# Storing transposed keys through SyncE with the output stores, and two full products placed between the last half-size products

## Chip, core and metric

The kernel runs on one core of a Trainium2 chip. The metric is the device time of one execution in microseconds. Three timed runs of the kernel before gave 1010.33, 1010.59 and 1010.79 us, median 1010.59.

## What is computed

The input `x` is 2 sequences of 2048 tokens of 512 elements in float32. Cut to what matters, the reference is:

```python
xn = layernorm(x)
z  = layernorm(xn) * gamma + beta                  # inside the attention
q, k, v = z @ qkv[:, :512], z @ qkv[:, 512:1024], z @ qkv[:, 1024:]
attn = softmax(causal(q @ k.T / sqrt(512)))        # each sequence by itself
s  = (attn @ v) @ o_proj + xn
top2 of (xn @ gate_w.T + gate_b + bias) over 8 experts, softmax of the two
y  = sum over the two: gate * (silu(xn @ w1[e].T + b1[e]) @ w2[e].T + b2[e])
out = x + s * silu(y)
```

## The kernel before

**Stages.** The work falls into three stages on one core. The first, 0 to 251 us in the profile, makes normalized tokens, keys, projected queries and projected values, and decides the routing to the experts. The second runs the experts over gathered tokens. The third is the causal attention with the gated output. The change touches the first stage only.

**Weights folded.** q and k appear only in q @ k.T, so the kernel forms `wqk`, the product of the query and key weights, once, and applies it to the transposed normalized tokens. These transposed tokens are what the program calls keys, `kT`. In the same way `wvo` is the product of the value weights and the output projection.

**Blocks.** The 4096 tokens are 8 blocks of 512 tokens. Of each block the first stage makes `kT` (four chunks of 128 x 512), a projected q and a projected v, and stores all three in DRAM (`kt_d`, `qt_d`, `v_d`), from where the attention reads them from 527 us on. The rows of a block are normalized on DVE, copied by POOL into 16-bit halves (`zu`), transposed by DMAs on SP's queue (`zuT`, L354), stored for the experts' gathers (`zu_d`, L357), and put together again by DVE as `zT` (L374); block 0 is transposed by PE instead. ACT then makes `kT` of `zT` in four steps (`scaled`, L379), and after the last of them issues one store of 1 MB from its own queue (L384). There are four `kT` buffers and one `zT` buffer.

**Products by seven.** Blocks 0 to 6 are projected with a scheme of seven half-size products for each q and each v, in place of eight. An item is the q or the v of one block, so there are 14 items, (0, q), (0, v), (1, q) and so on. `one_product(i, k)` (from L504) issues the eight 256-column matmuls of product k of item i (all at L526) and the ACT copies that follow it. The scheme accumulates in PSUM banks and passes partial sums between banks with ACT: product 1 goes to bank a, product 5 to bank d and from there to SBUF as the "fifth", product 2 adds to bank a, product 6 to bank b, which ACT copies to bank c (L555). Product 3 then adds to bank b, product 7 to bank c, and after bank c has been copied out (L539), product 4 adds to bank c. Two DVE adds per item (L395) bring the fifth to what products 3 and 7 gave; `deferred` holds an add back until two more products have been issued.

**Units.** Block 7 is projected with eight full products instead, the units (`unit(b, u)`, L439): four 512-column matmuls (L446 for q, L451 for v) into bank `(u + 1) % 4`, an ACT copy (L456) and an ACT store of 256 KB (L457).

**Order.** All engines run in the order in which the program issues. `chain_of_products` fixes the order of the products, interleaving an item with the next; of the last item only products 3, 7, 4 are left at the end, one directly after another. `pieces` is a generator that issues products and gives control back four times in seven products, 56 times in all, and then once per unit, 8 times. At each of these 64 steps other work is issued: `norm_*`, `keys`, gate products (`both`, L412) and their transposes (L427), loads of x and of the experts' weights, and from step 41 on the parts of `route`, the routing on DVE with its inversion matmuls on PE (`inv_p`, L746). `made` counts products; `scale_next` issues one waiting `scaled` step after a product. Stores of q and v of an item wait in the list `unstored` and are issued at the next product 3 (L577), through SP for blocks 0 to 4 and through ACT for blocks 5 and 6, or after a unit.

**SP's queue.** SP issues in one order the transposes, the `zu_d` stores, the loads of x and weights, and the q and v stores of blocks 0 to 4. An issue that has to wait holds up all those behind it.

Of the kernel before, what the change touches and what calls it, by code (L numbers as in the profile page):

```python
# [26 lines left out]
def gated_attention_moe(  # L27
# [28 lines left out]
    nc = tc.nc  # L56
    B, S, D = x.shape
    E, _, H = w1_t.shape
# [6 lines left out]
    ND = D // P  # L65
# [32 lines left out]
    kt_d = [dram.tile([P, ND, TB], F32, name=f"kt_d{b}") for b in range(NB)]  # L98
# [50 lines left out]
    banks = [ps_p.tile([P, TB], F32, name=f"bank_{k}", tag=f"bank_{k}") for k in "abcd"]  # L149
# [212 lines left out]
    def keys(b):  # L362
        zs = zs_of.pop(b)
        zT = ztp.tile([P, ND, TB], F32, name=f"zT_{b}", tag="zT")
        kT = kp.tile([P, ND, TB], F32, name=f"kT_{b}", tag="kT")
        if b < BY_TE:
            for c in range(ND):
                pt = ps_t.tile([P, TB], F32, name=f"pz_{b}_{c}", tag="pt")
                for t in range(BT):
                    nc.tensor.transpose(pt[:, ts(t, P)], zs[t][:, ts(c, P)], ident)  # L370
                nc.scalar.copy(zT[:, c, :], pt)
        else:
            for t in range(BT):
                nc.vector.tensor_copy(  # L374
                    zT[:, :, ts(t, P)].bitcast(U16).rearrange("p c (t h) -> p c t h", h=2),
                    zuts.pop((b, t)).rearrange("p (h c) t -> p c t h", h=2),
                )
        def scaled(c):
            nc.scalar.activation(  # L379
                kT[:, c, :], zT[:, c, :], AF.Identity,  # L380
                scale=gam[:, c : c + 1], bias=bet[:, c : c + 1],
            )
            if c == ND - 1:
                nc.scalar.dma_start(out=kt_d[b], in_=kT)  # L384

        wait = made[0] + {1: 3, NB - 1: 4}.get(b, 6)
        pending.extend((wait, scaled, c, b) for c in range(ND))
        kts[b], zts[b] = kT, zT

    made, pending, deferred = [0], [], []  # L390

    def add_due(wait=2):
        while deferred and deferred[0][0] + wait <= made[0]:
            _, f, args = deferred.pop(0)
            f(*args)  # L395

    def scale_next():
        if pending and pending[0][0] <= made[0]:
            _, f, c, _ = pending.pop(0)
            f(c)  # L400
# [38 lines left out]
    def unit(b, u):  # L439

        kT = kts[b]
        po = banks[(u + 1) % ND]
        r = u % ND
        for c in range(ND):
            if u < ND:
                nc.tensor.matmul(  # L446
                    po, lhsT=wqk[:, c, ts(r, P)], rhs=kT[:, c, :],
                    start=(c == 0), stop=(c == ND - 1),
                )
            else:  # L450
                nc.tensor.matmul(  # L451
                    po, lhsT=kT[:, c, ts(r, P)], rhs=wvo[:, c, :],
                    start=(c == 0), stop=(c == ND - 1),
                )
        o = stg.tile([P, TB], F32, name=f"j_{b}_{u}", tag="stg")
        nc.scalar.copy(o, po)  # L456
        nc.scalar.dma_start(out=(qt_d if u < ND else v_d)[b][:, r, :], in_=o)  # L457
# [4 lines left out]
    SEVEN = NB - 1  # L462
# [30 lines left out]
    items = [(b, of_q) for b in range(SEVEN) for of_q in (True, False)]  # L493
    FIFTH = {}

    def chain_of_products():
        yield from ((0, k) for k in (1, 5, 2, 6))
        for i in range(len(items)):
            more = i + 1 < len(items)
            for j, k in (1, 1), (0, 3), (0, 7), (1, 5), (0, 4), (1, 2), (1, 6):  # L500
                if j == 0 or more:
                    yield i + j, k

    def one_product(i, k):  # L504

# [61 lines left out]
        else:  # L567
# [1 line left out]
            nc.scalar.copy(place(1, 0), whole(bank_c))  # L569
            queue = nc.sync if b < LATE else nc.scalar  # L570
            unstored.extend(((qt_d if of_q else v_d)[b], g, outs[:, g], queue) for g in range(2))

    unstored = []

    def store(dst, g, src, queue):

        queue.dma_start(out=dst[:, 2 * g : 2 * g + 2, :], in_=src)  # L577
# [262 lines left out]
    units = [(b, u) for b in range(NB) for u in range(2 * ND)]  # L840
# [70 lines left out]

    def pieces():

        for n, (i, k) in enumerate(chain_of_products()):
            made[0] = n
            add_due()
            one_product(i, k)
            scale_next()
            if (n + 1) * 4 // 7 > n * 4 // 7:
                units.pop(0)  # L920
                yield
        while units:
            add_due(0)
            unit(*units.pop(0))
            while unstored:
                store(*unstored.pop(0))
            yield

    def sum_keys(i):
# [3 lines left out]
        elif i % (2 * ND) == 4 and b < SEVEN - 1:  # L933
            if b == 1:
                scale_all()
            key_sums(b)

    projected = pieces()
    for i in range(LAST + 1):
        next(projected)  # L940
# [347 lines left out]
    def maximum(s, src, at):  # L1288

        mx, _, pieces = scored[s]  # L1290
        nc.vector.tensor_reduce(mx[:, len(pieces) : len(pieces) + 1], src, AX.X, ALU.max)  # L1291
        pieces.append((src, at))
# [96 lines left out]
    def end_scores(s):  # L1389
        mx, nm, pieces = scored[s]  # L1390
        nc.vector.tensor_reduce(nm, mx[:, : len(pieces)], AX.X, ALU.max, negate=True)  # L1391
# [7 lines left out]
    while w2_left:  # L1399
# [12 lines left out]
        out=keep, in_=keep, compare_op=ALU.is_ge, fill=-HUGE,  # L1412
        base=0, pattern=[[-1, P]], channel_multiplier=1,
    )
    for i in range(NM):
# [21 lines left out]
        for _ in range(3):  # L1437
            if i >= paired.stop and early:
                f, b, c = early.pop(0)
# [316 lines left out]
    for s in range(NT + OUT + 2):  # L1756
# [7 lines left out]
        n = s // 2 + 1  # L1764
# [172 lines left out]
```

## Time and profile before

| what | value |
|---|---|
| median of the timed runs | 1010.59 us |
| time of the profiled execution | 1012.02 us |
| its span | 1010.3 us |
| granted PE clock | 1.00 |
| PE busy | 1001.5 us, 99% |
| DVE, POOL, ACT busy | 71%, 48%, 40% |
| waits of PE in the first 251 us | six, 4.2 us together |
| issues of kt_d stores | 8 on ACT, 1 MB each, 0.33 us each |

The profile is of one execution. Its rows name a line of the program, an engine, an operation, the tiles written and read (out<-in), the number of instructions, and the time. A timeline row begins with the start in us from the span's start and the duration; what stands in brackets at its end is the idle time of the engine before it, and whose work ended it. "ACTq" and "SPq" are those engines' sequencers, which issue DMAs. A wait row gives who waited for whom, the total in us, the number of times, and the longest. Ends of matmuls are modelled.

### The profile page before, as it was taken

Reading aid. Unit: us, or ns where it says so; the run is one execution under the profiler, and the core shown is the slowest. Engines: PE = TensorE matmul, PEld = TensorE weight load, DVE = VectorE, ACT = ScalarE, POOL = GpSimd, SP = SyncE. Lnnn points to the kernel's source line nnn. Section 1 sums busy time; section 2 is a strip of 40 time slices with the busy share of each in tenths; the row PEclk is TensorE's granted clock in tenths of the full one; section 3 lists DMA queues with packets and bytes.
Section 4 is the critical chain, followed back from the end, with each engine's and each line's share of the span. In section 5 each row is a group of like instructions: output and inputs, shape, how many; then the busy total and the mean of one; then the engine's idle time right before and its main releaser. Section 6 shows DMA issues by size and latency. Waiting matters only on the chain. (4 is left out here: it accounts for less than half of the span.)

```text
span 1010.3 us, 13408 instructions
## 1 busy us (share of the span) xinstructions
PE 1001.5 (99%) x3924; PEld 665.7 (66%) x3924; DVE 719.6 (71%) x1396; ACT 402.7 (40%) x804; POOL 481.6 (48%) x475
## 2 busy tenths in 40 slices
PE   9999999999999999999999999999999999999998
PEld 5887888874577677667653448677675544447577
DVE  6997755896877777776744669678576457878667
ACT  3354455322444544444455122232345544442241
POOL 4474465003744444443432256164557776764272
PEclk9999999999999999999999999999999999999999
DMA  8799987979999999999999576373677768753361
GB/s 291 234 240 319 319 237 268 331 254 230 182 247 213 205 219 218 210 211 214 213 213 254 162 191 149 90 189 110 186 199 233 224 202 241 204 146 86 95 164 42
DMA packets 295495, 207.96 MB, mean 206 GB/s; under 512 B 230648, under 2 KB 243704, under 8 KB 294400
## 3 DMA queue, kind: packets, MB, share of 16 engines
q1 hardware_dynamic: 280128, 155.17, 62.1%
q0 software_dynamic: 10400, 34.63, 12.6%
q10 hardware_dynamic: 4896, 17.30, 4.6%
q8 instruction: 34, 0.56, 0.2%
q14 instruction: 37, 0.30, 0.1%
HBM read 92.35 MB, written 60.03 MB: 151 GB/s over the span
## 5 line engine op out<-in xcount | busy, mean ns | idle before, releaser
L1191 PE MATMUL py<-arena,ht 128*128 (+3 forms) x396 | 176.7, 593 | 0.0
L1303 PE MATMUL ps<-k,q 128*128 128x512 f32 (+3 forms) x416 | 143.0, 495 | 0.3 <-PEq L1451 0.3
L1491 POOL COPY pu<-pT 128x1024 uint16<-128x1024 uint16 (+2 forms) x74 | 81.8, 1137 | 119.1 <-ACT pT L1481 59.2
L1162 POOL COPY hu<-h 128x704 uint16<-128x704 uint16 x66 | 61.8, 954 | 155.8 <-issue 121.7
L1191 PEld LDWEIGHTS py<-arena,ht 128*128 128x128 f32 (+3 forms) x396 | 71.8, 185 | 80.6 <-issue 76.4
L1303 PEld LDWEIGHTS ps<-k,q 128*128 128x128 f32 x416 | 74.7, 190 | 67.1 <-issue 56.3
L966 POOL DMA_INDIRECT xs<-zu_d,toki x66 | 77.7, 1177 | 70.6 <-DVE toki L793 55.9
L1177 ACT ACTIVATE ht<-ht,b1sel 128x128 f32<-128x128 f32 (+3 forms) x216 | 67.9, 380 | 88.4 <-DVE ht L1171 88.4
L1141 DVE TENSOR_TENSOR h<-p,h 128x176 f32<-128x176 f32 x182 | 55.4, 336 | 59.6 <-PE p L1134 56.1
L1674 POOL DMA_INDIRECT yg<-y_d,posi x64 | 67.3, 1052 | 36.9 <-DVE yg L1685 22.0
L1531 PE MATMUL po<-v,pT 128*128 128x512 f32 x152 | 67.9, 592 | 0.0
L347 POOL COPY zu<-z 128x1024 uint16<-128x1024 uint16 x32 | 39.4, 1230 | 57.7 <-DVE z L332 57.7
L1481 ACT ACTIVATE pT<-pT,nm 128x1024 f32<-128x1024 f32 x14 | 16.1, 1148 | 110.3 <-DVE nm L1391 72.0
L1513 DVE COPY pT<-puT 128x1024 uint16<-128x1024 uint16 (+2 forms) x74 | 53.4, 750 | 7.4 <-DMA puT<-pu 7.2
L1199 ACT COPY y<-py 128x512 f32<-128x512 f32 x55 | 32.1, 584 | 62.1 <-PE py L1191 48.2
L1481 ACT ACTIVATE pT<-ps,nm 128x512 f32<-128x512 f32 (+3 forms) x52 | 30.0, 580 | 60.4 <-DVE nm L1391 36.7
L1361 DVE TENSOR_TENSOR pT<-p,pT 128x512 f32<-128x512 f32 x49 | 32.9, 687 | 25.8 <-PE p L1355 22.1
L1531 PEld LDWEIGHTS po<-v,pT 128*128 128x128 f32 x152 | 28.6, 190 | 31.9 <-issue 30.1
L1042 DVE COPY xT<-xhT 128x1024 uint16<-128x1024 uint16 x66 | 44.7, 703 | 6.4 <-DMA xhT<-xs 6.3
L1703 POOL TENSOR_TENSOR o<-o,yg 128x512 f32<-128x512 f32 x30 | 41.4, 1380 | 14.3 <-DVE o L1695 14.2
L1695 DVE SCALAR_TENSOR_TENSOR o<-xo,xscale,o 128x512 f32<-128x512 f32 x30 | 25.9, 871 | 30.1 <-ACT o L1692 30.1
L1704 POOL TENSOR_TENSOR o<-o,xo 128x512 f32<-128x512 f32 x30 | 43.2, 1439 | 2.4
(342 smaller groups left out, 2146.9 us busy)
## 6 DMA issues: line engine op xcount, KB each, us to landing
y_d<-y SPq DMA_DIRECT2D x66, 256.0 KB, 4.3
zu_d<-zu SPq DMA_DIRECT2D x32, 264.0 KB, 3.2
kt_d<-kT ACTq DMA_DIRECT2D x8, 1024.0 KB, 8.2
q<-qt_d SPq DMA_DIRECT2D x32, 256.0 KB, 5.0
k<-kt_d SPq DMA_DIRECT2D x32, 256.0 KB, 4.2
v<-v_d SPq DMA_DIRECT2D x32, 256.0 KB, 5.7
xo<-in_x_dram SPq DMA_DIRECT2D x32, 256.0 KB, 4.0
x<-in_x_dram SPq DMA_DIRECT2D x30, 256.0 KB, 6.5
```

The costliest lines, as they stand in the source:

```text
L966: nc.gpsimd.indirect_dma_start(out=xs, out_offset=None, in_=zu_d, in_offset=bass.IndirectOffsetOnAxis(ap=toki[:, order[i] : order[i] + 1], ...
L1042: nc.vector.tensor_copy(xT.bitcast(U16).rearrange("p c (t h) -> p c t h", h=2), xhs.pop(i).rearrange("p (h c) t -> p c t h", h=2),)
L1141: nc.vector.tensor_tensor(out, x, y, ALU.add)
L1162: nc.gpsimd.tensor_copy(hu[:, :, :H], h.bitcast(U16).rearrange("p (d h) -> p h d", h=2))
L1177: nc.scalar.activation(ht[:hn, c, at], ht[:hn, c, at], AF.Silu, bias=b1sel[:hn, c, j : j + 1])
L1191: nc.tensor.matmul(py[at, :], lhsT=ht[:k, c, at], rhs=rhs[n], start=(c == 0), stop=(c == NH - 1),)
L1303: nc.tensor.matmul(ps[:, :w], lhsT=aqs[seq[s] // 2][:, c, ts(t % 2, P)], rhs=aks[first + j][:, c, :w], start=(c == 0), stop=(c == ND - 1),)
L1481: nc.scalar.activation(turned[s][:, at:end], src, AF.Exp, bias=nm, accum_out=rs[:, j : j + 1])
L1491: nc.gpsimd.tensor_copy(pu[:, : 2 * w].rearrange("p (h d) -> p h d", h=2), turned[s][:, k : k + w].bitcast(U16).rearrange("p (d h) -> p h ...
L1513: nc.vector.tensor_copy(turned[s][:, k : k + w].bitcast(U16).rearrange("p (i t h) -> p i t h", t=P, h=2), puT[:, : 2 * w // P, :].rearrang ...
L1531: nc.tensor.matmul(dst, lhsT=turned[s][:, ts(k, P)], rhs=avs[first + k // BT][:, k % BT, cols], start=(start and k == k0), stop=(k == k1 - 1),
L1674: nc.gpsimd.indirect_dma_start(out=y, out_offset=None, in_=y_d, in_offset=bass.IndirectOffsetOnAxis(ap=posi[k][:, n : n + 1], axis=0),)
```

## The change

Three things are different. First, `scaled` no longer issues the 1 MB store on ACT; it puts two stores of 512 KB into `unstored`, to be issued by SP together with the next q and v stores, whatever the block. Second, `chain_of_products` yields `None` twice among the products of the last item, ahead of its product 3 and ahead of its product 4; at each `None`, `pieces` issues the next unit of block 7 and gives control back. The products themselves and their number stay. Third, a unit uses bank `(u + 3) % 4`, so that unit 0 goes to bank d and unit 1 to bank a. The counter `n` is kept by hand, since units no longer all follow the products.

```diff
             if c == ND - 1:
-                nc.scalar.dma_start(out=kt_d[b], in_=kT)
+                unstored.extend((kt_d[b], g, kT[:, 2 * g : 2 * g + 2, :], nc.sync) for g in range(2))
...
-    made, pending, deferred = [0], [], []
+    made, pending, deferred, unstored = [0], [], [], []
...
-        po = banks[(u + 1) % ND]
+        po = banks[(u + 3) % ND]
...
     def chain_of_products():
         yield from ((0, k) for k in (1, 5, 2, 6))
-        for i in range(len(items)):
-            more = i + 1 < len(items)
+        for i in range(len(items) - 1):
             for j, k in (1, 1), (0, 3), (0, 7), (1, 5), (0, 4), (1, 2), (1, 6):
-                if j == 0 or more:
-                    yield i + j, k
+                yield i + j, k
+        for k in (None, 3, 7, None, 4):
+            yield len(items) - 1, k
...
-    unstored = []
...
-        for n, (i, k) in enumerate(chain_of_products()):
+        n = 0
+        for i, k in chain_of_products():
+            if k is None:
+                unit(*units.pop(next(j for j, (b, _) in enumerate(units) if b == SEVEN)))
+                yield
+                continue
             made[0] = n
             add_due()
             one_product(i, k)
             scale_next()
-            if (n + 1) * 4 // 7 > n * 4 // 7:
+            n += 1
+            if n * 4 // 7 > (n - 1) * 4 // 7:
                 units.pop(0)
                 yield
```

## The prediction

> **What bounds the kernel now.** I read the page first (engine totals, slices), then the waits of PE, then the timelines of PE, ACT, SP and DVE around each wait that the change touches.
>
> ```profile
> PE 1001.5 (99%) x3924; PEld 665.7 (66%) x3924; DVE 719.6 (71%) x1396; ACT 402.7 (40%) x804; POOL 481.6 (48%) x475
> ```
> ```profile
> PE bank_a L526 <- ACT raw L552: 1.4, 1, 1.4
> ...
> PE bank_b L526 <- ACT bank_c L555: 0.7, 1, 0.7
> PE inv_p L746 <- DVE which L779: 0.4, 1, 0.4
> ...
> PE bank_c L526 <- ACT so L539: 0.3, 1, 0.3
> ```
>
> PE is the bound in every stage: 99% busy at full clock, so only PE work or a PE wait is worth time. The change leaves the matmuls as they are; it can only move waits. All waits of PE are eight lines with one occurrence each, 4.9 us in all, and these four lie in the first 251 us, where the changed code runs. After 251 us PE has two waits, 0.4 us for DVE's work on PE's own results and 0.3 us of its own sequencer, so what PE gains before 251 us should reach the end.
>
> The listed idle understates a wait, because a product is drawn 1.89 us long while the next starts 1.73 us later (the tail overlaps). I price a wait by starts against the same pair elsewhere:
>
> ```profile
> 80.99 0.60 PE L427 MATMUL pgt<-ident,part 128*128 128x128 f32 x4
> 82.99 1.99 PE L526 MATMUL bank_a<-kT,wqk 128*128 128x256 f32 x8 [1.40 <-ACT raw L552]
> ...
> 212.72 1.89 PE L526 MATMUL bank_b<-arena 128*128 128x256 f32 x8
> 215.32 1.99 PE L526 MATMUL bank_b<-arena,kT 128*128 128x256 f32 x8 [0.71 <-ACT bank_c L555]
> 217.16 1.89 PE L526 MATMUL bank_c<-arena 128*128 128x256 f32 x8
> 218.88 0.64 PE L746 MATMUL inv_p<-which,at 128*128 128x136 bf16 x8
> 219.78 1.99 PE L526 MATMUL bank_c<-wvo,arena 128*128 128x256 f32 x8 [0.26 <-ACT so L539]
> ...
> 225.57 0.64 PE L746 MATMUL inv_p<-which,at 128*128 128x136 bf16 x8
> 226.63 0.63 PE L746 MATMUL inv_p<-which,at 128*128 128x136 bf16 x8 [0.43 <-DVE which L779]
> ```
>
> Without a wait, a product follows a gate transpose (L427) after 0.44 us (101.55 to 101.99), a product a product after 1.73, a product or an inversion an inversion after 0.47 (204.24 to 204.71). So the four cost 2.00 - 0.44 = **1.56**, 2.60 - 1.73 = **0.87**, 0.90 - 0.47 = **0.43** and 1.06 - 0.47 = **0.59** us.
>
> The first needs ACT's timeline:
>
> ```profile
> 76.49 0.81 ACT L379 ACTIVATE kT<-zT,bet,gam 128x512 f32<-128x512 f32 x1
> 81.49 0.33 ACTq L384 DMA_DIRECT2D kt_d<-kT  x1
> 81.86 0.58 ACT L569 COPY raw<-bank_c 128x512 f32<-128x512 f32 x1 [4.55 <-PE pgt L427]
> ```
>
> Block 2's keys were complete at 77.30, yet ACT issued their store at 81.49 and copied nothing meanwhile. PE L427 is not what it waited for: L384 reads nothing from PE. The trace's semaphore records show ACT held until 81.43 by one of eight DMA completion counters that SP and ACT use in turn; the last transfer on that counter was the third zu store, issued by SP at 77.05, last piece landed at 81.41 (SP's four x loads after it took 4.71 us to issue, against 1.79 at 24.9). PE's product needed bank_a, whose copy stands right behind the held one (82.34 to 82.94). So ACT paid for SP's congested queue, and PE for ACT.
>
> **The Trainium skill.** "PSUM — Partial Sum Buffer", Engine vs sequencer instructions: ScalarE's queue is strict FIFO. The trace agrees: the finished bank_c product waited for its copy until L384 was out (81.82, copy 81.86). Same page, PSUM bank collisions: a bank is guarded as a whole between TensorE and its reader; that is the 0.87 and 0.43 above. "DMA: Bandwidth & Descriptors", Issuing engines are not separate DMA queues: SP's and ACT's transfers share 16 engines, so moving the issuer saves only issue time. The trace agrees: from 85 to 86 us ACT's queue moved 385 KB and SP's 37. Same page, Rules for kernel authors: at least 1 MiB per DMA for full bandwidth. Here the halves do not show a loss: two 512 KB qt halves landed 1.30 us apart (72.03, 73.33), about 400 KB/us, as fast as the 1 MB stores.
>
> **Part 1: key stores moved to SP.** Removed from ACT: 8 issues of 0.33 us (2.6 us of an engine 40% busy, hidden by its idle time) and the one hold of 4.1 us, which is worth 1.56 us of PE. The other seven L384 issues follow their keys at once, so nothing is there to gain. Added to SP: 16 issues of 512 KB, at 0.58 us each (median of the L577 row) 9 us over 130 us. SP waits 53 us there for POOL's zu alone, so the issue time hides; without that cover it would delay the transposes by 1.2 us a block. Same bytes, 8 MB. A key buffer is written again four blocks later: block 1's (store landed near 75 at worst) at 131.4, so that wait stays hidden.
>
> What the stores are moved past is the question. They leave at the next third product of the chain, behind what SP has before it: block 0's store goes from 26.26 to about 62 (behind zuT and zu_d of block 2), block 1's from 53.56 to about 67, block 2's from 81.49 to about 96. So 2 MB more stand ahead of block 3's transposes (67.51 to 75.89). At the 390 KB/us that the trace's packets show in undisturbed stretches that is 5.4 us; at the 235 KB/us over 64.8 to 73.3 (2 MB landed) it is 8.9. The last zuT of block 3 landed at 79.41: it becomes 84.8 to 88.3, and with one copy of 0.7 to 1.7 us zT is ready at 85.5 to 90.0. PE's gate product of block 3 (L412, 88.37 before) would come at 86.8. Cost 0 to 3.2 us; nothing below zero, as PE cannot start it earlier. I take 0, since block 1's store also leaves the queue at 54 to 57 and SP's issue is spread. From block 4 on the zT copies wait for ACT (97.96, with zuT landed at 95.74), and block 2's 1 MB has left the stretch 81 to 89, so the backlog is repaid.
>
> **Part 2: two units between the last products.** Nothing is removed: the same 8 units of block 7 run, two of them earlier. Unit 0 goes on bank_d (read out at 209.5), unit 1 on bank_a (213.5), so both start at once; each covers 3.49 us. In the clock of before: unit 0 at 214.45, inversion 217.94, products 218.41 and 220.14, inversion 221.87, unit 1 222.34, inversions 225.83 and 226.30, last product 226.77, unit 2 at 228.5. Product 3 needs ACT's bank copy (done 215.3), product 4 the copy of bank_c (about 222.5): 0.87 and 0.43 go, covered by the units. The inversion wait goes too: its `which` needed 3.2 us after the inversion at 221.61 and an add of 0.69 (222.73) stood before it; now it starts at 222.4 without the add and is ready at 225.7, before 226.30. Next late is nothing on PE. Extra changes of operand shape: up to 0.1 us, taken as 0.
>
> Moved with them: two ACT copies and two qt_d stores (0.33 each), ACT being idle over 1 us before each product's copy, and block 6's two qt_d stores, which leave at the third product, 3.1 us later; nobody reads them before 527. Block 7's keys were complete at 170. The counter of products, by which adds fall due, doesn't count units. W2's last loads wait for products 7 and 4, so SP issues them at 222 and 228.6 instead of 219.08 and 221.80; SP's next transpose starts at 232.30 in any case. First expert product: xT was joined at 242.45, needed at 249.2.
>
> The add of product 7 now falls behind the router's DVE block:
>
> ```profile
> 222.73 0.69 DVE L395 TENSOR_TENSOR so<-so,p 128x512 f32<-128x512 f32 x1
> ...
> 227.31 0.30 DVE L788 COPY inv<-inv_p 128x136 f32<-128x136 f32 x1 [0.72 <-PE inv_p L746]
> ```
>
> That block lasts 14.29 us (to 241.60, the end of DVE L833); starting at 227.0 the add ends near 242.0. The second v_d store waits for it on ACT, from about 232.5, and behind it the copies of units 3 to 5. Unit 7 needs unit 3's bank at 245.7, and the copy ends near 243.0: 2.7 us to spare, cost 0.
>
> **Sum.** 1.56 + 0.87 + 0.43 + 0.59 = 3.45 us. The profiled execution: 1012.02 (span 1010.3 plus 1.7 around it) - 3.45 = 1008.57. The three timed runs have a median 1.43 below the profiled time, so **1007.1**. Within 0.2% (2.0 us) is about what a measurement here can't tell from no change.
>
> **Rivals.**
> - *Backlog or no stall to save*: the 1.56 is given back at L412, or the timed runs don't have it (the 1.43 between profile and median would fit). For: DMA share over 1.0 from 60 to 110 us. Against: three runs within 0.46 us. Gain 1.89: 1008.7.
> - *Tail shifted, not gained*: `which` is ready only 0.6 us before its use; if the inversions wait there again, and the backlog takes the 1.56, a third of the tail's 1.89 is left, 0.6: 1010.0. For: DVE is over 90% busy there. Against: DVE's work moves with PE's, and an add falls out of its way.
> - *Slower, by ACT parked*: the second v_d store, at 242.0, also has to get a completion counter. If that wait is over 2.7 us, unit 7 stands still. The longest of this kind is SP's 8.1:
>
> ```profile
> SPq L955 <- DMA v_d<-arena: 8.1, 1, 8.1
> ```
>
>  That costs 5.4 us, net +1.95: 1012.5. Against: ACT met such a hold once in its 24 stores.
>
> **Chances.** Full gain 0.50 (own range 1006.5 to 1007.8); backlog 0.27; shifted 0.11; slower 0.12. Faster by over 0.2%, below 1008.6: the first and 0.12 of the second, 0.62; within 0.2%: 0.15 + 0.11 = 0.26; slower 0.12. Range: 1006.5 to 1010.2 leaves out the slower case and a little of the others.
>
> **What would show it.** ACT has no gap at 77 to 82 and PE no wait for bank_a; PE's waits lose L555, L539 and L779; unit 0 and 1 appear on bank_d and bank_a among the last products; a v_d store leaves ACT near 240. I am wrong if PE waits for zT at L412, or for a unit's copy before 250 us, or if the four waits go and the span does not follow.

## The result, and the profile after

The changed kernel took 1008.2 us (median of 10 runs, 1007.43 to 1008.87), beside 1010.75 us for the kernel before (10 runs, 1010.33 to 1013.08). The ratio is 0.997 with a 95% interval of 0.9962 to 0.9978: faster by 2.55 us by the medians and by 3.0 by the ratio. The forecast was 1007.1 with a range of 1006.5 to 1010.2: the direction and the range held, and the point was 1.1 us too low. The profiled execution of the changed kernel took 1007.83 us with a span of 1006.0, where the one before took 1012.02 and 1010.3.

The engine totals on the page after:

```profile
PE 999.9 (99%) x3924; PEld 665.3 (66%) x3924; DVE 716.9 (71%) x1396; ACT 403.2 (40%) x804; POOL 483.3 (48%) x475
```

PE has the same 3924 matmuls and is as full as before. All of its waits (who waited for whom, total, times, longest) are now four:

```profile
PE warm L870 <- DVE b1s L181: 1.1, 1, 1.1
PE p L1583 <- DVE u L1600: 0.4, 1, 0.4
PE ps L1307 <- PEq L1455: 0.3, 1, 0.3
PE pz L370 <- ACT zT L371: 0.3, 1, 0.3
```

The four that the prediction priced are gone, and no new one took their place. PE's timeline after shows the two places:

```profile
80.43 0.60 PE L427 MATMUL pgt<-ident,part 128*128 128x128 f32 x4
80.87 1.89 PE L526 MATMUL bank_a<-kT,wqk 128*128 128x256 f32 x8
...
86.15 1.06 PE L412 MATMUL pg<-zT,gw 128*32 128x512 f32 x8
...
212.23 3.60 PE L446 MATMUL bank_d<-kT,wqk 128*128 128x512 f32 x8
215.66 0.64 PE L744 MATMUL inv_p<-which,at 128*128 128x136 bf16 x8
216.13 1.94 PE L526 MATMUL bank_b<-arena,kT 128*128 128x256 f32 x8
217.91 1.89 PE L526 MATMUL bank_c<-arena 128*128 128x256 f32 x8
219.64 0.64 PE L744 MATMUL inv_p<-which,at 128*128 128x136 bf16 x8
220.11 3.65 PE L446 MATMUL bank_a<-kT,wqk 128*128 128x512 f32 x8
223.60 1.11 PE L744 MATMUL inv_p<-which,at 128*128 128x136 bf16 x16
224.54 1.94 PE L526 MATMUL bank_c<-wvo,arena 128*128 128x256 f32 x8
...
243.49 3.60 PE L451 MATMUL bank_c<-wvo,kT 128*128 128x512 f32 x8
```

The product into bank_a follows the gate transpose by 0.44 us, where it took 2.00. The gate product that might have met the backlog (L412) starts at 86.15 with no wait in brackets. In the tail the units stand on bank_d and bank_a, and every start follows the one before it within 0.06 us of what the sum had drawn: the two inversions at 223.60 run as one group of 16 matmuls. Unit 7, the last, starts at 243.49.

ACT's timeline after, first around the keys of block 2, then around the parked v_d store:

```profile
75.94 0.82 ACT L379 ACTIVATE kT<-zT,bet,gam 128x512 f32<-128x512 f32 x1
77.18 0.59 ACT L569 COPY raw<-bank_c 128x512 f32<-128x512 f32 x1 [0.43 <-PE bank_c L526]
78.91 0.59 ACT L552 COPY raw<-bank_a 128x512 f32<-128x512 f32 x1 [1.14 <-PE bank_a L526]
...
230.95 9.05 ACTq L575 DMA_DIRECT2D v_d<-so  x2
240.05 0.59 ACT L456 COPY j<-bank_c 128x512 f32<-128x512 f32 x1 [9.51 <-DVE so L395]
```

Copies now follow the keys within half a microsecond; before, ACT stood from 77.30 to 81.49. And ACT is parked in the tail: it stands at the two v_d stores for 9.05 us, 8.3 of them waiting for DVE's add (`so`, L395) as foreseen; its copy of unit 3 (bank_c) ends at 240.64, and unit 7 needs that bank at 243.49.

**Where the time went.** I compared the start of each matmul with its start before. The two profiled spans differ by 4.3 us: 0.55 in the first 7 us, 1.67 at the bank_a product and 2.05 in the tail; after that the offset stays the same to the end. The first part is no work of the change. PE's timelines of before and then of after, at the first products with weights:

```profile
4.06 2.08 PE L225 MATMUL bank_a<-raw 128*128 128x512 f32 x2
5.92 1.19 PE L225 MATMUL bank_b<-raw 128*128 128x512 f32 x2
```
```profile
4.18 1.51 PE L225 MATMUL bank_a<-raw 128*128 128x512 f32 x2
5.53 1.02 PE L225 MATMUL bank_b<-raw 128*128 128x512 f32 x2
```

Within these rows PE waits for nothing; the matmuls themselves come closer together in the changed kernel. The third follows the second after 0.85 us before and after 0.43 in the changed kernel. The record of the granted clock in the traces begins full speed at 6.25 us in the one and at 5.00 in the other. In the fourteen executions profiled for this document that moment lies between 4.17 and 7.34 us, and the fifth of these matmuls starts between 5.92 and 7.54, the later the later full speed begins (correlation 0.997). The same program differs in this too: 6.25 and 5.60 us in the two executions of before. So the change itself is worth 1.67 + 2.05 = 3.72 us in this pair of profiles (3.45 predicted), and 2.55 to 3.0 in the timed runs.

### The profile page after: what moved, and what is told of

It is laid out like the page before. It is cut to its first block, busy times and chain, and to the rows that moved or that the text cites. A ratio compares the mean times of both kernels' runs of the same rounds, so it can differ in the third digit from the quotient of the medians.

```text
span 1006.0 us, 13431 instructions
## 1 busy us (share of the span) xinstructions
PE 999.9 (99%) x3924; PEld 665.3 (66%) x3924; DVE 716.9 (71%) x1396; ACT 403.2 (40%) x804; POOL 483.3 (48%) x475
## 5 line engine op out<-in xcount | busy, mean ns | idle before, releaser
L1365 DVE TENSOR_TENSOR pT<-p,pT 128x512 f32<-128x512 f32 x49 | 32.9, 687 | 25.8 <-PE p L1359 22.1
```

## The experiments

**The theory** is the prediction's: key stores on ACT now and then wait for a DMA completion counter that SP's transfers still hold (called a hold below), which stops ACT's copies and through them PE; and the units cover three waits in the tail. **Rivals**: the gain is all in one part; it is the later time or the half size of the key stores that helps, not the issuer; ACT's parking in the tail is itself a cost or a danger.

### Each part alone, and the kernel before again

keys_only is the kernel before with only the key stores moved (units stay at the end); units_only is the changed kernel with the store back on ACT (the units keep their new banks, which no run tried apart):

```diff
-                unstored.extend((kt_d[b], g, kT[:, 2 * g : 2 * g + 2, :], nc.sync) for g in range(2))
+                nc.scalar.dma_start(out=kt_d[b], in_=kT)
```

block2_only moves only the one store that was held, and before_again is the kernel before with nothing changed, for a second profile.

```diff
-                nc.scalar.dma_start(out=kt_d[b], in_=kT)
+                if b == 2:
+                    unstored.extend((kt_d[b], g, kT[:, 2 * g : 2 * g + 2, :], nc.sync) for g in range(2))
+                else:
+                    nc.scalar.dma_start(out=kt_d[b], in_=kT)
```

keys_only: 

> Only the key stores go to SP with the next output stores; units stay behind the last product. Theory (one hold of ACT behind block 2's store, 1.6 us of PE): 1.6 us faster than before, PE's wait for bank_a gone, the three waits of the tail (0.7, 0.3, 0.4 us listed) still there. Rival (the hold was a chance of the one profiled execution): 0 to 0.5 us faster when timed. Rival (SP's backlog costs something elsewhere): PE waits at the gate products of blocks 3 to 5, slower than before.

units_only: 

> Only the two units move between the last products, on the new banks; the key stores stay on ACT. Theory: 2.0 us faster than before (0.87 + 0.43 + 0.59 by the starts of before, 2.05 by those of after), bank_a's wait near 82 us still there in the profile. Rival (the whole timed gain comes from here, as the hold was a chance): as fast as the changed kernel, 2.6 to 3 us.

block2_only: 

> The kernel before, with block 2's key store alone moved to SP behind the next output stores; the other seven stay on ACT. Theory (only that store was ever held): 1.6 us faster, as keys_only, and no wait of PE for ACT before 200 us. Rival (ACT's issues cost in every block): clearly less than keys_only. Rival (the hold passes to another of ACT's stores, since the order of the completion counters shifts): a new wait of PE at another block, 0 to 1 us faster.

before_again: 

> The kernel before, unchanged, one more execution with a profile. Theory: PE waits again for bank_a near 82 us, 1 to 2 us, and the three waits of the tail return within 0.1 us. Rival (the hold was a chance): no wait for bank_a, and a span about 1.5 us shorter.

| kernel | median us (runs) | before beside it | ratio, 95% interval | span of the profile |
|---|---|---|---|---|
| keys_only | 1009.92 (14) | 1010.95 | 0.9998, 0.9986 to 1.001 | 1008.5 |
| units_only | 1009.05 (13) | 1010.95 | 0.9981, 0.9973 to 0.9989 | 1007.4 |
| block2_only | 1010.36 (13) | 1010.95 | 0.9994, 0.9986 to 1.0002 | 1008.7 |
| before_again | 1011.14 (1) | | | 1009.4 |

The units alone gain 1.9 us, as the sum for the tail had it (1.89). keys_only is undecided: its median is 1.0 us lower, but four of its fourteen runs took 1012 to 1016 us and pulled the ratio to 1; of the 35 runs of before beside it, four took 1012 to 1013. In its profile the wait for bank_a is gone and the tail's three waits are still there. block2_only is undecided too; its profile has no bank_a wait either, and before 200 us no wait for ACT but the 0.3 us at `pz` that every profile has, so in this execution none of the other seven stores cost PE anything. It lost 0.1 us at 122 us and some 0.5 at the experts' entrance, where DVE waits 3.4 us for a transpose (`huT`), against 2.7 before; why that landed later I did not trace.

The useful finding came from the profiles that keep the stores on ACT. ACT's timeline in units_only:

```profile
80.60 0.33 ACTq L384 DMA_DIRECT2D kt_d<-kT  x1
80.97 0.58 ACT L569 COPY raw<-bank_c 128x512 f32<-128x512 f32 x1 [3.93 <-PE bank_b L526]
```

The hold is there again at the same store. PE's product starts 1.37 us after the gate transpose (80.72 to 82.09) and in before_again 1.34 (80.77 to 82.11), so the hold costs 0.93 and 0.90 us there, against 1.56 in the profile that the prediction was made from. It is there in all three profiles that have block 2's store on ACT at its old place. By the semaphore records of all three, ACT waits for the same counter, last used by the third zu store of SP, and is released within 0.03 us of that store's last landing: at 81.41, 80.54 and 80.52 us. The size of the hold changes from execution to execution, and the first profile had a large one.

### The keys alone once more

keys_again repeats keys_only on another chip.

> The kernel with the key stores alone moved, a second time, since four of its 14 runs lay over 1012 and left the interval at no verdict. Theory: 0.9 to 1.2 us faster than before (the hold of PE was 0.9 in two of three profiles of kernels with ACT's stores, 1.6 in the third). Rival (the moved stores bring a slow case of their own): again a quarter of the runs over 1012, which the kernel before shows in a seventh.

It took 1010.35 us in 22 runs (1009.41 to 1011.07) beside 1011.2 in 27 runs: 0.999, interval 0.9984 to 0.9997. The key stores are worth about 0.9 to 1.0 us, which agrees with a cost of 0.90 to 0.93, or 1.0 with the slower start after the wait (below). The runs over 1012 us did not come back. The two parts add up: 1.0 + 1.9 = 2.9, against 2.55 to 3.0 for both.

### Issuer, delay or half size

sp_at_once is the kernel before with the same 1 MB store at the same place in the program, on SP instead of ACT. act_later is the changed kernel with late half stores, but issued by ACT:

```diff
-                nc.scalar.dma_start(out=kt_d[b], in_=kT)
+                nc.sync.dma_start(out=kt_d[b], in_=kT)
```
```diff
-                unstored.extend((kt_d[b], g, kT[:, 2 * g : 2 * g + 2, :], nc.sync) for g in range(2))
+                unstored.extend((kt_d[b], g, kT[:, 2 * g : 2 * g + 2, :], nc.scalar) for g in range(2))
```

sp_at_once: 

> The kernel before, with each block's 1 MB key store issued by SP in the place where ACT issued it, not later and not in halves. Theory (the issuer matters, since SP's own holds lie beside PE's work): no wait of PE for bank_a, 0.9 to 1.6 us faster than before, as keys_only. Rival (SP reaches the store before the keys are there, waits for ACT, and block transposes queue behind it): PE waits at gate products, 0 to 3 us slower than before.

act_later: 

> The changed kernel, with the key stores still in halves and still at the next product 3, but issued by ACT. Theory (the issuer matters): ACT is held again at one or more of these stores by a completion counter that SP's transfers use, and PE waits 0.3 to 2 us somewhere in 60 to 170 us. Rival (the later place is what helps, whoever issues): no such wait, as fast as the changed kernel.

sp_at_once took 1010.11 us (20 runs) beside 1011.19: 0.9987, interval 0.998 to 0.9993, the gain of the keys without delay and without halves. Its PE has no wait for bank_a, although SP now stands waiting for keys (PE's timeline, and waits of SP's queue):

```profile
80.96 0.60 PE L427 MATMUL pgt<-ident,part 128*128 128x128 f32 x4
81.39 1.89 PE L526 MATMUL bank_a<-kT,wqk 128*128 128x256 f32 x8
```
```profile
SPq L384 <- ACT kT L379: 6.6, 2, 4.6
```

PE lost some 0.5 us at the experts' entrance instead, in a wait of 0.2 for ACT's `ht`, as in block2_only.

act_later took 1014.01 us (13 runs) beside 1011.19: 1.0027, interval 1.0016 to 1.0038, slower than the kernel before although it keeps the gain of the tail. ACT's timeline there, and then PE's:

```profile
59.22 0.57 ACT L560 COPY bank_b<-bank_a 128x512 f32<-128x512 f32 x1
63.06 1.23 ACTq L575 DMA_DIRECT2D kt_d<-kT  x2
64.33 0.59 ACT L539 COPY raw<-bank_c 128x512 f32<-128x512 f32 x1 [4.53 <-DMA zu_d<-zu]
```
```profile
60.13 1.89 PE L526 MATMUL bank_d<-arena 128*128 128x256 f32 x8
64.97 1.99 PE L526 MATMUL bank_c<-wvo,arena 128*128 128x256 f32 x8 [2.95 <-ACT raw L539]
```

Here the bracket itself names the cause: what ended ACT's 4.53 us was a landing of `zu_d`, a store issued by SP that has nothing to do with the keys. PE starts 4.84 us after the product before it instead of 1.73: 3.1 us lost, and 1.0 more at 106 us, where the counter was last used by a qt_d store of SP. With 0.1 for the slower start after each wait the two make 4.3 of the 4.9 us between its span (1010.9) and that of the changed kernel; 0.3 more is the first matmuls' clock and 0.3 a gate transpose at 171 us. So the gain needs neither delay nor half size, and on ACT the same late halves are worse. The issuer is the cause.

### The parked store: how far from harm, and what if it is not parked

In the tail ACT is parked behind the second v_d store, which waits for DVE's add. add_late delays that add by filler work on DVE ahead of the remaining units; add_early issues the add ahead of the router's work, so that the store is not parked:

```diff
+        for _ in range(17):
+            nc.vector.tensor_tensor(sc, sc, sc, ALU.min)
         while units:
```
```diff
             one_product(i, k)
+            if (i, k) == (len(items) - 1, 4):
+                add_due(0)
             scale_next()
```

add_late: 

> The changed kernel, with 17 more operations of DVE (a minimum of the routing scores with themselves, which changes nothing, about 0.4 us each, 6.8 us in all) between the router's last DVE block and the add of product 7. Theory (from 2.85 us on, each us that the add is later stops PE at unit 7): PE waits about 3.9 us for a unit's copy near 244 us, span 3.9 us longer than the changed kernel's. Rival (ACT has more room than that, or the first experts' tokens, joined by DVE behind the add, decide): 0 to 1.5 us longer, with PE's wait at the first expert product.

add_early: 

> The changed kernel, with the add of the last item's product 7 issued right behind product 4, ahead of the router's last DVE block. Theory (ACT's 9 us behind the second v_d store lie inside unit 7's slack of 2.85 us): ACT's hold from 230.95 to 240.00 is gone, PE's schedule is the same, the time that of the changed kernel within 0.3 us. Rival (the parked ACT costs something that the waits of PE don't list): 0.3 to 1 us faster than the changed kernel.

add_late took 1016.82 us (4 runs, 1015.28 to 1019.74; the profiled one is the shortest) beside 1011.19: 1.0059, interval 1.0038 to 1.0079. Its timelines of ACT and of PE, and PE's last windows (length; busy us of PE, PEld, DVE, ACT and POOL with instructions; granted clock share; DMA share; GB/s):

```profile
231.78 16.75 ACTq L575 DMA_DIRECT2D v_d<-so  x2
248.57 0.58 ACT L456 COPY j<-bank_c 128x512 f32<-128x512 f32 x1 [17.20 <-DVE so L395]
```
```profile
240.88 3.60 PE L451 MATMUL bank_b<-wvo,kT 128*128 128x512 f32 x8
249.21 5.36 PE L451 MATMUL bank_c<-wvo,kT 128*128 128x512 f32 x8 [4.73 <-ACT j L456]
254.41 7.85 PE L1088 MATMUL ph<-w,xT 128*128 x26
```
```profile
249.00:256.00 7.00, 6.79 (x14) 3.33 (x15) 1.73 (x3) 2.50 (x5) 1.14 (x3) 0.76 0.78 262
```

This execution runs 0.82 us behind the changed kernel's ahead of the filler (240.88 against 240.06). Counted from there, ACT's copy comes 7.7 us later and unit 7 starts 4.9 later, so the first 2.8 us of delay are free; the prediction had 2.7 to spare. The mechanism of the slower rival is real, and the changed kernel stands 2.8 us from it. Beyond that the price is more than the wait: the experts' first product comes 6.7 us later, 1.8 more than the 4.9, because PE came out of the wait at a reduced rate (window row, clock 0.76; unit 7 drawn as 5.36 us instead of 3.60). The expectation of 3.9 us in all did not foresee this.

add_early took 1008.68 us (10 runs, 1007.62 to 1010.56) beside 1011.19: 0.9973, interval 0.9963 to 0.9983. That is not better than the changed kernel's 0.997, and its runs spread: five lie between 1007.6 and 1008.3, three between 1010.1 and 1010.6, two between these. Its profile is of a long one (1010.38). ACT's timeline, and PE's wait:

```profile
231.61 1.76 ACTq L575 DMA_DIRECT2D v_d<-so  x2
...
240.93 0.59 ACT L456 COPY j<-bank_a 128x512 f32<-128x512 f32 x1 [2.85 <-PE bank_a L451]
249.97 0.33 ACTq L457 DMA_DIRECT2D v_d<-j  x1
250.39 0.59 ACT L456 COPY j<-bank_b 128x512 f32<-128x512 f32 x1 [8.88 <-PE ph L1088]
```
```profile
PE py L1197 <- ACT ht L1183: 1.4, 2, 1.0
```

The long park at 231 is gone, and ACT stands 8.4 us later on: the store behind the copy of 240.93 leaves at 249.97. By the trace's semaphore records its counter belonged to one of SP's transposes of the experts' tokens, issued at 234.97 and landed at 249.9. Behind it ACT comes late to the experts' activations, and PE loses 2.0 us at 258 and 264. The five transposes are slower there, too; SP's queue in the changed kernel, and in add_early:

```profile
229.93 11.76 SPq L1041 DMA_TRANSPOSE xhT<-xs  x5
```
```profile
230.45 19.72 SPq L1043 DMA_TRANSPOSE xhT<-xs  x5
```

### Both once more

> The kernel with the early add, unchanged, one more execution with a profile. Its ten timed runs lay half near 1008 and half near 1010. Theory (a hold of ACT behind a store of block 7 near 241 to 250 us, present in some executions, makes the difference): near 1008 without the hold and without a wait of PE for ht, or near 1010 with both. Rival: near 1010 with no hold, or near 1008 with one.

> The changed kernel, unchanged, one more execution with a profile. Theory: PE has no wait for bank_a, bank_b, bank_c and inv_p, the tail is as in the first profile within 0.1 us, and what differs in the span lies in the first 7 us, where the weights arrive. Rival (other holds of ACT come and go in it, as in add_early): a wait of PE for ht or a bank of 0.5 to 2 us.

Each ran once more. add_early_again took 1010.55 us, again a long one, and ACT's timeline again has the hold, this time with the transposes named in the bracket:

```profile
244.18 0.59 ACT L456 COPY j<-bank_a 128x512 f32<-128x512 f32 x1 [6.15 <-DMA xhT<-xs]
248.24 0.33 ACTq L457 DMA_DIRECT2D v_d<-j  x1
248.66 0.59 ACT L456 COPY j<-bank_b 128x512 f32<-128x512 f32 x1 [3.89 <-DMA xhT<-xs]
```

PE lost 1.25 us at the experts' entrance and 0.9 in the attention. after_again took 1007.70 us with the same four waits of PE, and every start within 0.15 us of the first profile after. So both profiles of add_early have the hold and neither profile of the changed kernel does. That the shorter runs of add_early are those without a hold is likely but not shown, since no profile fell on one.

The other profiles bear on this too. In the five with a parked store (units_only, act_later, add_late and both of the changed kernel) no unit's store leaves more than 0.3 us after its copy. Of the nine without it, five have a unit's store held by a counter of the experts' transposes, for 0.7 us (sp_at_once), 2.9 (block2_only), 5.8 and 8.4 (add_early twice) and 11.6 (one_unit, below); four have none, among them both of before.

### One unit instead of two

one_unit leaves out the second `None`, so that only unit 0 stands among the last products:

```diff
-        for k in (None, 3, 7, None, 4):
+        for k in (None, 3, 7, 4):
```

> The changed kernel with only one unit moved, ahead of product 3; product 4 follows product 7 and one inversion again. Theory (a wait goes only where 3.4 us of other work stand in it, and DVE's pace sets the inversions): the wait before product 3 is gone (about 1.0 us), the 0.3 us before product 4 is back, and the last inversion, now right behind product 4, waits 1 to 1.6 us for `which`; the tail as a whole gains 0 to 0.3 us of the 2.05. Rival (each unit takes away the wait it stands in, and the inversion's wait goes with the first): about 1.5 us of the 2.05 are gained.

It ran once: 1015.82 us. Neither theory said that. The waits in the tail went as far as its one unit covers: product 3's is gone, product 4 waits 0.2 us for ACT and an inversion 0.68 for `which`; 0.80 of the 2.05 us was gained, between the 0 to 0.3 of the theory and the 1.5 of the rival. The loss lies behind. ACT's timeline, and two windows of PE (columns as above):

```profile
235.02 0.59 ACT L456 COPY j<-bank_c 128x512 f32<-128x512 f32 x1 [1.47 <-PE bank_c L446]
247.24 0.33 ACTq L457 DMA_DIRECT2D qt_d<-j  x1
247.60 0.59 ACT L456 COPY j<-bank_d 128x512 f32<-128x512 f32 x1 [12.00 <-DMA xhT<-xs]
```
```profile
256.00:262.00 6.00, 2.98 (x10) 1.67 (x10) 1.37 (x3) 2.26 (x5) 4.96 (x5) 0.99 0.95 243
262.00:268.00 6.00, 6.00 (x13) 2.82 (x13) 6.00 (x8) 2.55 (x7) 3.17 (x3) 0.73 0.89 187
```

A unit's store was held 11.6 us by a counter of the transposes. PE lost 3.3 us waiting for the experts' activations (`ht`), 1.8 more at the reduced clock after that wait, and about 1.4 in smaller ones around it. So the cost of ACT's stores in the tail depends on which counter each of them draws, that is, which of the eight comes next in turn; with one unit the draw was bad. What one_unit does in most executions is open, as this is one.

## Why the prediction was right, and where its point was off

The range held, but it reached from the full gain to nearly no change (1010.2), so that alone says little. The measured 1008.2 lies above the 1006.5 to 1007.8 that the prediction gave to the full gain. What speaks for it is the signs that it named: the four waits are gone, the units stand on bank_d and bank_a, a v_d store leaves at 240.0, and PE waits neither at L412 nor for a unit.

**Keys, 1.56 us: mechanism right, size too large.** The sum took the hold from the single profiled execution. In the two other profiles with the same store on ACT it cost 0.90 and 0.93, and by timed runs the part is worth 0.9 to 1.0. This term is the one that was mis-sized, by about 0.6 us. The 0.1 by which the profile shows more (1.67) is the start after the wait, which is slower too (below). The rival that the timed runs don't have the 1.56 was therefore right in part: they have about 0.9 to 1.0 of it. And that moving the issuer saves only issue time, as the prediction says, is too narrow here: ACT's issue time was hidden, and the move alone (sp_at_once) gained 1.1 to 1.3 us, since the hold went with it.

**From profile to median, 1.43 us: the same error seen again.** With this constant the forecast comes to 1010.59 - 3.45: a stall measured in a long execution was taken off the median of the timed ones. Part of what made that execution long was the large hold itself: before_again's was 0.88 us shorter, 0.66 of it in the hold (1.56 against 0.90) and 0.22 at the first matmuls, where full clock came earlier. With 0.9 in place of 1.56 the sum is 2.8 us; taken from the median of 1010.75 beside which the result was measured, it gives 1007.95, where 1008.2 was found.

**Tail, 0.87 + 0.43 + 0.59 = 1.89: right.** The profile shows 2.05 and the runs of units_only 1.9. The 0.16 that the profile shows beyond the sum is the slower start after each wait, which falls away with the wait.

**Backlog, taken as 0: right, though not for a reason that is shown.** The key stores left SP at 61, 67 and 96 us as foreseen. Block 3's transposes landed at 80.25, 0.8 us later than before and earlier than the 84.8 to 88.3 of the estimate. Over 64.8 to 73.3 us SP's queue moved 367 KB/us by its packets, where it had moved 246 before. ACT's queue moved nothing there in either trace, so it is not what made the difference, and the cause stays open. The gate product came at 86.15 (86.8 foreseen) without a wait. DVE waited 1.0 us for a transpose once, and PE waited for neither. The rival that gives the 1.56 back there is refuted.

**Half-size stores: the conclusion held, the reading did not.** The prediction took 400 KB/us from two landings 1.30 us apart, but the time between two landings is not a rate: from 71 to 73 us, just before the second landing, the queue moved only 122 KB. The packets of the two halves went mostly from 67 to 71 us, and from 68 to 70 the queue moved 395 KB/us. That halves lose nothing is better seen from the runs: 0.9987 with 1 MB stores on SP (sp_at_once) and 0.999 with halves (keys_again), with intervals that overlap.

**Parked store, taken as 0 with 2.7 us to spare: right.** The slack is 2.8 us by add_late. The store left at 240.0, 2 us before the estimate. The Trainium skill, "DMA: Bandwidth & Descriptors", Anatomy of one DMA, says that any semaphore wait of a DMA happens on the issuing sequencer before dispatch. The section is on DMAs that GpSimd issues; the traces show the same for stores that ACT issues. ACT was idle for 4.55 us in the profile before, 4.53 in act_later and 12.00 in one_unit, and each time copies that were ready stood behind the store. What the prediction did not see is that the park may do something useful: it sends the units' stores out from 240 on, when SP's transposes are nearly all issued (229.93 plus 11.76 us). The five profiles with the park have no later hold, and five of the nine without it do; that the park is what prevents the hold is argued from this, not shown, and the four others show that its absence alone does not bring a hold. No run gave ACT counters of its own, so whether that would bring both gains was not tried.

**Tail shifted, not gained:** refuted, the inversions wait for nothing. The part of that rival that one would get with less cover is what one_unit shows: with one unit the inversion still waits 0.68 us.

## What to carry to other kernels

A store issued by a compute engine costs that engine more than its 0.33 us whenever it must wait, for its data or for a completion counter that another engine's transfer still holds; everything queued behind it waits too, so look for the gap ahead of a DMA issue, not at its length. Move such a store to an engine that computes nothing, or place it where the next work of its engine has slack, and test what that slack is. A stall that depends on DMA landings has to be read from more than one execution before it goes into a sum, and its size in one long execution must not be taken off the median of others.

## What the runs showed of the hardware

- After a wait, the first matmul costs PE about 0.1 us more: the first two matmuls of the product stood 0.32 us apart instead of 0.21. The four waits that went gave 0.27 us beyond their priced length (0.11 at bank_a, 0.16 in the tail).
- After waits of 3.0 (one_unit) and 4.7 us (add_late) the next four 512-column matmuls came 0.76 to 1.01 us apart instead of 0.43, 1.8 us more in all. The clock records show half speed for 3.41 us in both, from 261.87 and from 249.17 us. After act_later's 2.95 us the rate was full (64.97 to 66.80). The Trainium skill, "TensorE: Matmul & The Clock Gate", HAM oscillation, puts the limit for PE gaps at about 3.4 us. By the listed idle time one at 3.0 is already over; from the last start before the wait to the first after it the three are 3.48, 5.33 and 3.33 us. These agree with the page, but three cases don't fix a limit.
- At the start the same matmuls came 0.85 us apart until the clock record shows full speed, and 0.43 after it. That moment lay between 4.17 and 7.34 us in the fourteen profiled executions and moved all that follows.
- Five DMA transposes of the experts' tokens took SP from 10.6 (act_later) to 22.1 us (one_unit) from the first issue to the end of the last, waits between them included; in the changed kernel 11.8 and 11.5, before 14.6 and 17.5. One of them alone held SP for 1.2 to 6.7 us.
